# Single-row fetches shared between SyncE and ScalarE: twelve gathers instead of eight leave GpSimd, in step with the recurrence

## The chip, the cores and the metric

The kernel runs on one core of a Trainium2 chip. A core has five engines that run on their own and meet at semaphores: TensorE (PE in the profile) for matrix products, VectorE (DVE), ScalarE (ACT), GpSimd (POOL) and SyncE (SP), which here only issues transfers. SP and ACT issue plain transfers, each on a queue of its own, and GpSimd issues gathers; the bytes are moved by 16 DMA engines. The metric is the device time of one execution in microseconds. Time before: median 1851.0 us of three runs (1845.76 to 1854.84).

## The reference

A table `emb` has 100001 rows of 128 numbers; row 0 counts as zero. There are 1024 sequences of 50 item numbers, and a length for each.

```python
e = emb[seq]                              # (1024, 50, 128)
prefix = cumsum(e, axis=1)
denom = minimum(t_idx[None, :], lengths[:, None])
uF = prefix / denom[:, :, None]
y = (uF - uF.mean(axis=0)) * rsqrt(uF.var(axis=0) + BN_EPS) * gamma + beta
def step(v, x):                           # over the 50 places of the sequence
    v = v + (x - v) / 2
    spike = (v >= 1)
    return v - spike, spike
scores = mean_of_spikes @ emb.T           # (1024, 100001), float32
```

So there are 50 steps, each of which needs 1024 rows of the table at data-dependent places, and then one large product whose result, 410 MB, has to be written out.

## The kernel before

*Two stages.* The first stage is the loop over the 50 steps (line 383), with the state laid out as 128 features on the partitions by 1024 sequences. The second (line 546) goes over the table in pieces of 1024 rows, turns each piece round on PE, splits it into a high and a low part, multiplies it with the spike counts, and stores the scores. The second stage is untouched by the change. Most of the table pieces that the second stage begins with are fetched during the first one: `held` = 6 groups of 6 pieces and 4 more, 40 pieces of 512 KB, and of these 38 by SP at its very start (lines 231 to 238; the other two late, at line 473).

*One step.* `gather(t)` (line 244) fetches the 1024 rows of step t as eight indirect DMAs of 128 rows, issued by GpSimd into a tile `e` that has two buffers. `gather(t + 2)` stands behind step t's use of the buffer, so GpSimd can be two steps ahead, and then waits for PE. PE transposes the eight blocks of `e` and adds them onto the running sum `pre` in PSUM (line 390), after a small correction for row 0 (line 348). DVE makes the mean so far (`uF`, line 401) and its statistics (lines 402 and 410). ACT takes the square root of the variance (line 414) and centres `uF` (line 421), DVE finishes the reciprocal root (lines 427 to 440), ACT applies it (line 444), DVE makes the new potential `v` (line 447), and ACT writes `d`, the potential less the threshold (line 360), for the next step's reset. The square root of line 414 occurs once in each step, so its times give the periods of the steps.

*Rows by SP.* In the eight steps of `BY_SYNC` the last of the eight gathers is left out, and its 128 rows come by plain transfers of one row (512 bytes) each: `fetch_singles` (line 260) loads 32 row addresses into registers (line 265) and issues 32 transfers (line 268), four times over, into one of four banks of `held_rows`. PE takes that bank in place of the last block of `e` (line 392). The call for the next of these steps stands behind the use of the one before, in step order, but SP itself has nothing in its stream that ties it to the step, other than that a bank must have been read before it is filled again, four fetches later.

*What sets the order.* Each engine runs its own instructions in the order in which the program was written; the framework adds the semaphores. The completion of the transfers that SP and ACT issue is counted in eight semaphores, handed out in turn over both engines in the order of the program, and a transfer is issued only after the one that had its semaphore before, the eighth before it, has landed. GpSimd's gathers have eight of their own.

Of the kernel before, what the change touches and what calls it, by code (L numbers as in the profile page):

```python
# [17 lines left out]
U8 = mybir.dt.uint8  # L18
# [3 lines left out]
P = 128  # L22
# [4 lines left out]
BANK = 512  # L27
GROUP = 6
AHEAD = 6
# [3 lines left out]
SHIFT = TWICE + ASIDE  # L33
FURTHER = {5: 1, 6: 2}

BY_SYNC = (11, 17, 22, 28, 33, 38, 43, 48)
AT_ONCE = 32

SPARED = 120
PICKED = range(42, 97, 3)  # L40
# [7 lines left out]
def rec_kernel(  # L48
# [9 lines left out]
    nc = tc.nc  # L58
    B, T = seq.shape
    N, D = table.shape  # L60
    NB = B // P
# [16 lines left out]
    held_rows = const.tile([P, BANK], F32, tag="countB", name="held_rows")  # L78
# [16 lines left out]
    def pair(i):  # L95
        free.append([embp.tile([P, HALF], F32R, tag=f"{x}{i}", name=f"{x}_{i}") for x in ("hi", "lo")])

    def size(q):
        return min(HALF, N - q * HALF)
# [4 lines left out]
    def group(g):  # L104
        at = g if g < AHEAD else AHEAD - 2 + g % 2
        r = rowp.tile([P, GROUP, HALF], F32, tag=f"rows{at}", name=f"rows_{g}")
        for k in range(GROUP):
            rows[g * GROUP + SHIFT + k if g else k + ASIDE * (k >= TWICE)] = r[:, k, :]
        return r
# [19 lines left out]
    def pick(r, q, engine):  # L129
        j = PICKED.index(q)  # L130
        rows_of(r[:SPARED, :], picks, j)
        if j % 2:
            engine.dma_start(out=r[SPARED:, :], in_=runs[q * P + SPARED : (q + 1) * P, :])
            turn_by(TURN)
        else:
            turn_by(4)
            rows_of(r[SPARED:, :], ends, j // 2)
            turn_by(5)

    def fetch(r, k, q, n):  # L140

        engine = nc.sync if q < held else nc.scalar
        n = min(n, parts - q)
        whole = n - (size(q + n - 1) < HALF)
        wide = whole - (whole == n and q + whole - 1 in PICKED)
        if wide:
            engine.dma_start(
                out=r[:, k : k + wide, :],
                in_=table[q * HALF : (q + wide) * HALF, :].rearrange("(q p k) d -> p q (k d)", p=P, k=KQ),
            )  # L150
        if wide < whole:
            pick(r[:, k + wide, :], q + wide, engine)
        if whole < n:
            full, rest = divmod(size(parts - 1), KQ)
            c1 = (parts - 1) * HALF
            r = r[:, k + whole, :]
            if rest:
                at = full - full % 32
                nc.vector.memset(r[at : at + 32, :], 0.0)
                engine.dma_start(  # L160
                    out=r[full : full + 1, : rest * D],
                    in_=table[c1 + full * KQ : N, :].rearrange("(o k) d -> o (k d)", o=1),
                )
            if full:
                engine.dma_start(
                    out=r[:full, :],
                    in_=table[c1 : c1 + full * KQ, :].rearrange("(p k) d -> p (k d)", k=KQ),
                )
# [19 lines left out]
    def prepare(q, pt):  # L188
        turned(q, pt)
        split[q] = hi, lo = free.pop(0)  # L190
        vp, vh, vl = views(q, pt, hi, lo)
        nc.scalar.copy(vh, vp)  # L192
        nc.vector.tensor_tensor(vl, vp, vh.bitcast(F32), ALU.subtract)  # L193
# [18 lines left out]
    with ExitStack() as ph:  # L212
# [21 lines left out]
            rows[TWICE + k] = spare[:, k, :]  # L234
        fetch(spare, 0, TWICE, ASIDE)
        fetch(first, TWICE, SHIFT, GROUP - TWICE)
        for g in range(1, AHEAD):
            fetch(group(g), 0, g * GROUP + SHIFT, GROUP)

        es = {}

        def gather(t):
            es[t] = gp.tile([P, B], F32, tag="e", name=f"e_{t}")
            for n in range(NB - (t in BY_SYNC)):
                nc.gpsimd.indirect_dma_start(  # L247
                    out=es[t][:, n * P : (n + 1) * P],
                    out_offset=None,
                    in_=table,  # L250
                    in_offset=bass.IndirectOffsetOnAxis(ap=idx[:, n, t : t + 1].bitcast(U32), axis=0),
                )

        byte_rows = table.rearrange("n d -> (n d)").bitcast(U8)
        row_bytes = 4 * D
        starts = ids[:T, :P].bitcast(I32)
        regs = [nc.sync.alloc_register(f"row{k}") for k in range(AT_ONCE)]
        singles = {}

        def fetch_singles(i):  # L260
            t = BY_SYNC[i]
            rows_of = held_rows[:, i % (BANK // P) * P :][:, :P]
            singles[t] = rows_of
            for p0 in range(0, P, AT_ONCE):
                nc.sync.load(regs, starts[t : t + 1, p0 : p0 + AT_ONCE])  # L265
                for k, reg in enumerate(regs):
                    at = nc.sync.snap(reg, donate=True, min_val=0, max_val=(N - 1) * row_bytes)
                    nc.sync.dma_start(  # L268
                        out=rows_of[p0 + k : p0 + k + 1, :].bitcast(U8),
                        in_=byte_rows[bass.ds(at, row_bytes)].rearrange("(o b) -> o b", o=1),  # L270
                    )

        make_identity(nc, ident)
        isz = up.tile([P, NB, P], F32, tag="uF", name="isz")
        rb = up.tile([P, NB, P], F32, tag="uF", name="rb")
        gather(0)

        last_ids = ids[:, P : P + T]
        nc.vector.tensor_copy(last_ids, idx[:, NB - 1, :])
        ips = vp.tile([P, B], F32, tag="v0", name="ips")  # L280
        nc.tensor.transpose(ips[:T, :P], last_ids, ident)
        nc.vector.tensor_scalar_mul(starts, ips[:T, :P], float(row_bytes))
        fetch_singles(0)

        nc.vector.memset(isz, 0.0)
        for u in (0, P // 2):
# [46 lines left out]
        def only(t):  # L333

            k = t % ONLY
            if k == 0:
                n = min(ONLY, T - t)
                nc.vector.tensor_tensor(
                    ls[:, :n, :],
                    r0n.unsqueeze(1).to_broadcast([P, n, D]),  # L340
                    sel[:, t : t + n].unsqueeze(2).to_broadcast([P, n, D]),
                    ALU.mult,
                )
            return ls[:, k, :]
# [12 lines left out]
        def over(t, v):  # L357

            d = lp.tile([P, B], BF16, tag="d", name=f"d_{t}")
            nc.scalar.activation(d, v, AF.Identity, bias=less)  # L360
            return d
# [4 lines left out]
        def spiked(out, cs, v):  # L366
            nc.vector.scalar_tensor_tensor(out, v, V_TH, count[:, cs], ALU.is_ge, ALU.add)
# [15 lines left out]
        for t in range(T):  # L383
# [18 lines left out]
                nc.vector.bn_stats(bs[:, h, :], uF[:, cs])  # L402
            if t + 2 < T:
                gather(t + 2)
            if t in BY_SYNC[:-1]:
                fetch_singles(BY_SYNC.index(t) + 1)
            if not last:
                correct(t + 1, l)
            mv = sp.tile([P, 2], F32, tag="mv", name=f"mv_{t}")
# [3 lines left out]
            r = sp.tile([P, 1], F32, tag="r", name=f"r_{t}")  # L413
# [29 lines left out]
            def x(vt, cs):  # L443
                nc.scalar.activation(vt, uF[:, cs], AF.Identity, bias=hgb[:, 1:2], scale=a)

            def step(vt, cs):
                nc.vector.scalar_tensor_tensor(vt, negv[:, cs], -0.5, vt, ALU.mult, ALU.add)  # L447

            if not last:
                vt = vp.tile([P, B], F32, tag=f"v{(t + 1) % 2}", name=f"v_{t}")  # L450
                x(vt, whole)
                if t:
                    spiked(count, whole, v)
                step(vt, whole)
                v = vt
                if t == T - 2:
                    spiked(count, whole, v)
                    moved = once.tile([P, P], F32, tag="r0hi", name="moved")
                    nc.vector.tensor_scalar_add(moved, v[:, pieceA], beta2)
                    near = once.tile([P, P], F32, tag="r0", name="near")  # L460
                    nc.vector.scalar_tensor_tensor(near, v[:, pieceA], V_TH, moved, ALU.is_ge, ALU.subtract)
                d = over(t, v)
                if t + 2 < T:
                    l = only(t + 2)

                if t in (T - 8, T - 6):
                    q = (t - T + 8) // 2
                    pair(q)
                    prepare(q, vp.tile([P, HALF], F32, tag="v0", name=f"pt_{q}"))
                    if q == TWICE - 1:  # L470
                        for k in range(TWICE):
                            rows[GROUP + ASIDE + k] = first[:, k, :]
                        nc.sync.dma_start(
                            out=first[:, :TWICE, :],
                            in_=table[(GROUP + ASIDE) * HALF : (GROUP + SHIFT) * HALF, :].rearrange(
                                "(q p k) d -> p q (k d)", p=P, k=KQ
                            ),
                        )

# [64 lines left out]
    for c, W in enumerate(WIDTHS):  # L546
# [38 lines left out]
        for n, q in blockwise:  # L585
# [4 lines left out]
            o = os[n]  # L590
# [27 lines left out]
            if n in (1, 4) and c >= MIDDLE and to_fetch < parts:  # L618
                g, k = divmod(to_fetch - SHIFT, GROUP)
                if k or to_split >= (g - 1) * GROUP + SHIFT:  # L620
                    if k == 0:
                        r = group(g)
# [23 lines left out]
```

## Time and profile before

| | |
|---|---|
| median of the runs | 1851.0 us (1845.76, 1851.0, 1854.84) |
| the profiled execution | 1852.0 us, its span 1850.0 us |
| mean granted clock of TensorE | 0.763 |
| busy over the span: PE, DVE, ACT, POOL | 58%, 51%, 36%, 23% |
| gathers of line 247 | 392 |
| single-row transfers of line 268 | 1024, by SP |
| HBM read, written | 77.69 MB, 409.60 MB |

How to read it. The page cuts the span into 40 slices and gives the busy share of each engine in tenths. A group's row has its line, engine and operation, the tiles that it writes and reads, how often it ran, its busy time and the mean of one, and the time that its engine stood before it with what ended that. A row for one line gives the shortest, median and longest of its instructions in ns and the first and last start in us. A wait's row gives who waited for whom, the total in us, how often, and the longest. A stretch's row gives, after its length, busy us and counts of PE, PEld, DVE, ACT and POOL, then the granted clock, the busy share of the DMA engines and the GB/s that they moved. A row in order of time gives start and duration in us; SPq and ACTq are the queues on which SP and ACT issue transfers.

### The profile page before, as it was taken

What the parts mean: (1) busy time and instruction counts of PE and PEld (TensorE: products, weight loads), DVE (VectorE), ACT (ScalarE), POOL (GpSimd) and SP (SyncE); (2) the same over time, 40 slices, a digit from 0 to 9 for tenths busy, and PEclk for the clock granted to TensorE, in tenths of its full rate; (3) what the DMA queues carried; (4) which work ended last, traced back from release to release, by engine and by line L of the source; (5) the groups of instructions that cost most, each with busy time, mean ns of one, the idle gap of its engine ahead of it and who ended that gap; (6) DMA issues with size and microseconds to landing.
All of it is one profiled execution on the core that took longest, in us unless ns stands there. A gap on an engine that the chain in (4) does not pass through costs nothing.

```text
span 1850.0 us, 14486 instructions
## 1 busy us (share of the span) xinstructions
PE 1070.6 (58%) x4465; PEld 810.4 (44%) x4465; DVE 947.7 (51%) x1128; ACT 674.2 (36%) x698; POOL 429.7 (23%) x459
## 2 busy tenths in 40 slices
PE   3321302120212213088998988878888878888984
PEld 2110201010101112066676766666666666666763
DVE  4653707261524346175566655555555555555652
ACT  2331303130312123054555544444444444444542
POOL 6664716262716254200000000010010010000000
PEclk7555555555555555589999999999889899989998
DMA  9511101010201011069999999999999999999999
GB/s 351 178 44 28 49 15 46 21 48 16 50 14 45 17 41 32 15 266 413 405 422 402 431 421 426 425 427 428 426 427 427 426 427 428 423 422 429 427 428 391
DMA packets 54993, 488.27 MB, mean 264 GB/s; under 512 B 12719, under 2 KB 14000, under 8 KB 33796
## 3 DMA queue, kind: packets, MB, share of 16 engines
q1 hardware_dynamic: 32944, 431.39, 55.4%
q0 software_dynamic: 16560, 35.40, 6.6%
q10 hardware_dynamic: 5412, 20.56, 2.7%
q8 instruction: 35, 0.57, 0.1%
q14 instruction: 42, 0.34, 0.1%
HBM read 77.69 MB, written 409.60 MB: 263 GB/s over the span
## 4 chain that ended last, share of the span: by engine, by line
DMA 33%; PE 15%; DVE 4%; ACT 3%; SPq 3%; issue 3%; ACTq 0%; DVEq 0%
DMA scores<-o 33%; PE po L200 15%; DVE o L601 2%; ACT o L603 2%; SPq L268 2%; DVE pairs L193 1%; ACT pairs L192 1%; PE pt L176 0%; SPq L265 0%; ACT hi L192 0%; DVE lo L193 0%; DVE bs L402 0%; DVE uF L401 0%; DMA held_rows<-in_L_rec_emb_table 0%; ACTq L603 0%
## 5 line engine op out<-in xcount | busy, mean ns | idle before, releaser
L601 DVE TENSOR_SCALAR o<-po 128x1024 f32<-128x1024 f32 (+1 forms) x390 | 467.2, 1214 | 309.6 <-DMA scores<-o 163.7
L603 ACT ACTIVATE o<-po 128x1024 f32<-128x1024 f32 x392 | 393.2, 1025 | 490.7 <-DMA scores<-o 337.2
L247 POOL DMA_INDIRECT e<-in_L_rec_emb_table,idx x392 | 372.9, 951 | 377.2 <-PE pre L390 218.6
L200 PE MATMUL po<-pairs,countB 128*128 128x512 f32 (+1 forms) x1120 | 289.9, 404 | 47.8 <-ACT o L603 47.6
L200 PE MATMUL po<-pairs,countC 128*128 128x512 f32 (+1 forms) x840 | 243.9, 438 | 62.3 <-ACT o L603 55.4
L401 DVE SCALAR_TENSOR_TENSOR uF<-rlen,pre 128x512 f32<-128x512 f32 x100 | 67.9, 679 | 399.0 <-PE pre L390 317.2
L200 PEld LDWEIGHTS po<-pairs,countB 128*128 128x128 f32 x1120 | 208.3, 191 | 110.9 <-ACT o L603 64.9
L200 PEld LDWEIGHTS po<-pairs,countC 128*128 128x128 f32 x840 | 169.8, 210 | 115.9 <-ACT o L603 66.0
L348 PE MATMUL pre<-zT,ls 128*128 128x512 f32 x100 | 78.5, 787 | 227.3 <-DVE uF L401 136.7
L390 PE MATMUL pre<-ident,held_rows 128*128 128x128 f32 x8 | 3.6, 447 | 349.2 <-DMA held_rows<-in_L_rec_emb_table 349.2
L414 ACT ACTIVATE r<-mv,eps 128x1 f32<-128x1 f32 x50 | 14.8, 295 | 509.2 <-DVE mv L410 406.3
L122 POOL DMA_INDIRECT rows<-in_L_rec_emb_table,picks x19 | 18.6, 981 | 685.2 <-PE pt L176 681.9
L390 PEld LDWEIGHTS pre<-ident,held_rows 128*128 128x128 f32 x8 | 1.5, 183 | 351.7 <-issue 351.7
L348 PEld LDWEIGHTS pre<-zT,ls 128*128 128x128 f32 x100 | 29.4, 295 | 267.4 <-DVE uF L401 159.3
L193 DVE TENSOR_TENSOR pairs<-pt,pairs 128x1024 fp32r<-128x1024 f32 x70 | 85.3, 1218 | 98.0 <-ACT pairs L192 97.1
L390 PE MATMUL pre<-ident,e 128*128 128x128 f32 x392 | 101.3, 422 | 19.2 <-DMA e<-in_L_rec_emb_table,idx 12.7
L176 PE MATMUL pt<-ident,rows 128*128 128x128 f32 (+1 forms) x768 | 104.9, 282 | 9.3 <-DVE v L447 5.0
L176 PEld LDWEIGHTS pt<-ident,rows 128*128 128x128 f32 (+1 forms) x768 | 94.3, 147 | 26.3 <-issue 10.8
L390 PEld LDWEIGHTS pre<-ident,e 128*128 128x128 f32 x392 | 81.6, 219 | 37.4 <-DMA e<-in_L_rec_emb_table,idx 18.9
L200 PE MATMUL po<-hi,countB 128*128 128x512 f32 x208 | 84.8, 408 | 10.8 <-ACT o L603 9.2
L192 ACT CAST pairs<-pt 128x1024 fp32r<-128x1024 f32 x70 | 70.0, 1012 | 39.2 <-PE pt L176 39.2
L200 PE MATMUL po<-lo,countB 128*128 128x512 f32 x208 | 83.3, 401 | 0.0
(99 smaller groups left out, 1110.1 us busy)
## 6 DMA issues: line engine op xcount, KB each, us to landing
scores<-o SPq DMA_DIRECT2D x96, 3072.0 KB
scores<-o SPq DMA_DIRECT2D x32, 1536.0 KB
scores<-o SPq DMA_DIRECT2D x29, 1024.0 KB
scores<-o SPq DMA_DIRECT2D x8, 2896.5 KB
rows<-in_L_rec_emb_table ACTq DMA_DIRECT2D x19, 1024.0 KB
held_rows<-in_L_rec_emb_table SPq DMA_DIRECT2D x1024, 0.5 KB
rows<-in_L_rec_emb_table SPq DMA_DIRECT2D x5, 3072.0 KB
e<-in_L_rec_emb_table,idx POOLq DMA_INDIRECT x392
```

Of the source, the lines that this page charges most:

```text
L122: nc.gpsimd.indirect_dma_start(out=r, out_offset=None, in_=runs, in_offset=bass.IndirectOffsetOnAxis(ap=which[: r.shape[0], j : j + 1].bit ...
L176: nc.tensor.transpose(pt[:, k0 : k0 + pw], r[:pw, k0 : k0 + D], ident[:pw, :pw])
L192: nc.scalar.copy(vh, vp)
L193: nc.vector.tensor_tensor(vl, vp, vh.bitcast(F32), ALU.subtract)
L200: nc.tensor.matmul(po[:, :kw], lhsT=counts[n], rhs=part[:, k0 : k0 + kw], start=j == 0, stop=j == 1,)
L247: nc.gpsimd.indirect_dma_start(out=es[t][:, n * P : (n + 1) * P], out_offset=None, in_=table, in_offset=bass.IndirectOffsetOnAxis(ap=idx[: ...
L268: nc.sync.dma_start(out=rows_of[p0 + k : p0 + k + 1, :].bitcast(U8), in_=byte_rows[bass.ds(at, row_bytes)].rearrange("(o b) -> o b", o=1),)
L348: nc.tensor.matmul(pre[h], lhsT=l, rhs=zT[:, h * BANK : (h + 1) * BANK], start=t == 0, stop=False, skip_group_check=True,)
L390: nc.tensor.matmul(pre[h][:, k : k + P], lhsT=singles[t] if h * BANK + k + P == B and t in singles else e[:, h * BANK + k : h * BANK + k + P],
L401: nc.vector.scalar_tensor_tensor(uF[:, cs], rlen[:, cs], 1.0 / (t + 1), pre[h], ALU.max, ALU.mult)
L601: nc.vector.tensor_scalar_mul(o[:, h0 : h0 + hw], po[:, :hw], 1.0 / T)
L603: nc.scalar.mul(o[:, h0 : h0 + hw], po[:, :hw], 1.0 / T)
```

## The change

Twelve steps instead of eight leave their last gather out: 6, 10, 14 and so on to 46, and 49. Their rows are cut into batches of 32, four for each such step, 48 in all, and one batch is issued at the end of each of steps 0 to 47: SP loads 22 addresses and issues 22 rows, ACT loads 10 addresses and issues 10 rows, and in the program's order they stand in turns, SP, ACT, SP, ACT, until ACT's ten are through. Of the table pieces only groups 0 and 1 and the two pieces set aside are fetched at the start; groups 2 to 5 become 24 parts of one piece each, and SP issues one behind each of the first 24 batches. The batch of a step stands behind everything else of that step: on ACT behind the activation of line 360, and ahead of the next step's square root. In step 44 it stands behind the load of line 473.

```diff
-BY_SYNC = (11, 17, 22, 28, 33, 38, 43, 48)
-AT_ONCE = 32
+APART = (*range(6, 47, 4), 49)
+STARTED = 0
+SYNC_ROWS, OWN_ROWS = 22, 10
+EARLY = 2
...
-        for g in range(1, AHEAD):
+        for g in range(1, EARLY):
             fetch(group(g), 0, g * GROUP + SHIFT, GROUP)
+        parts_left = []
+        for g in range(EARLY, AHEAD):
+            r = group(g)
+            parts_left += [(r, k, g * GROUP + SHIFT + k, 1) for k in range(GROUP)]
...
-            for n in range(NB - (t in BY_SYNC)):
+            for n in range(NB - (t in APART)):
...
-        regs = [nc.sync.alloc_register(f"row{k}") for k in range(AT_ONCE)]
+        sync_regs = [nc.sync.alloc_register(f"row{k}") for k in range(SYNC_ROWS)]
+        own_regs = [nc.scalar.alloc_register(f"own{k}") for k in range(OWN_ROWS)]
...
-        def fetch_singles(i):
-            t = BY_SYNC[i]
-            rows_of = held_rows[:, i % (BANK // P) * P :][:, :P]
-            singles[t] = rows_of
-            for p0 in range(0, P, AT_ONCE):
-                nc.sync.load(regs, starts[t : t + 1, p0 : p0 + AT_ONCE])
-                for k, reg in enumerate(regs):
...
+        def fetch_row(engine, reg, row):
+            at = engine.snap(reg, donate=True, min_val=0, max_val=(N - 1) * row_bytes)
+            engine.dma_start(
+                out=row.bitcast(U8),
+                in_=byte_rows[bass.ds(at, row_bytes)].rearrange("(o b) -> o b", o=1),
+            )
+
+        def fetch_some(i, p0):
+            t = APART[i]
+            rows_of = singles[t] = held_rows[:, i % (BANK // P) * P :][:, :P]
+            p1 = p0 + SYNC_ROWS
+            nc.sync.load(sync_regs, starts[t : t + 1, p0:p1])
+            nc.scalar.load(own_regs, starts[t : t + 1, p1 : p1 + OWN_ROWS])
+            for k, reg in enumerate(sync_regs):
+                fetch_row(nc.sync, reg, rows_of[p0 + k : p0 + k + 1, :])
+                if k < OWN_ROWS:
+                    fetch_row(nc.scalar, own_regs[k], rows_of[p1 + k : p1 + k + 1, :])
+
+        todo = [(i, p0) for i in range(len(APART)) for p0 in range(0, P, SYNC_ROWS + OWN_ROWS)]
...
-        fetch_singles(0)
...
-            if t in BY_SYNC[:-1]:
-                fetch_singles(BY_SYNC.index(t) + 1)
...
+                if t >= STARTED and todo:
+                    fetch_some(*todo.pop(0))
+                    if parts_left:
+                        fetch(*parts_left.pop(0))
```

More of the change, by code (lines that the diff above doesn't have):

```diff
@@ L256, in rec_kernel @@
         starts = ids[:T, :P].bitcast(I32)
-        regs = [nc.sync.alloc_register(f"row{k}") for k in range(AT_ONCE)]
+        sync_regs = [nc.sync.alloc_register(f"row{k}") for k in range(SYNC_ROWS)]
+        own_regs = [nc.scalar.alloc_register(f"own{k}") for k in range(OWN_ROWS)]
         singles = {}
-        def fetch_singles(i):
-            t = BY_SYNC[i]
-            rows_of = held_rows[:, i % (BANK // P) * P :][:, :P]
-            singles[t] = rows_of
-            for p0 in range(0, P, AT_ONCE):
-                nc.sync.load(regs, starts[t : t + 1, p0 : p0 + AT_ONCE])
-                for k, reg in enumerate(regs):
[L267 to L271, printed above, removed]
+        def fetch_row(engine, reg, row):
[15 more added lines that the diff above has]
+        todo = [(i, p0) for i in range(len(APART)) for p0 in range(0, P, SYNC_ROWS + OWN_ROWS)]
         make_identity(nc, ident)
```

## The prediction

> **What bounds the kernel now.** I read the slices of the page first, then the groups and waits of the step stage, then the row transfers of line 268 in stretches.
>
> ```profile
> span 1850.0 us, 14486 instructions
> DVE  4653707261524346175566655555555555555652
> POOL 6664716262716254200000000010010010000000
> DMA  9511101010201011069999999999999999999999
> L414 ACT ACTIVATE r<-mv,eps 128x1 f32<-128x1 f32 x50 | 14.8, 295 | 509.2 <-DVE mv L410 406.3
> ```
>
> A slice is 46 us. From slice 17 on DMA is full: that is the stage of products and stores, which the change leaves alone. Before it stand fifty steps in which DMA is nearly idle, and DVE and POOL stop several times together, in holes a slice or two wide. The ends of this stage come from the square root that every step has once on ACT:
>
> ```profile
> L414 ACT ACTIVATE r<-mv,eps x50: 294/295/298, 22.5 to 798.2; 128x1 f32<-128x1 f32 x50
> 789.04 0.30 ACT L414 ACTIVATE r<-mv,eps 128x1 f32<-128x1 f32 x1 [42.19 <-DVE mv L410]
> ```
>
> Step 0 is at 22.5, step 48 at 789.0, step 49 at 798.2 us. The 48 periods between step 0 and step 48 take (789.0 - 22.5)/48 = 16.0 us each. What they wait for is in the table of waits and in the record of line 268:
>
> ```profile
> PE pre L390 <- DMA held_rows<-in_L_rec_emb_table: 349.2, 8, 50.5
> POOL e L247 <- PE pre L390: 218.6, 10, 36.7
> SPq L268 <- DMA held_rows<-in_L_rec_emb_table: 5.7, 12, 0.8
> L268 SPq DMA_DIRECT2D held_rows<-in_L_rec_emb_table x1024: 1/228/5427, 42.0 to 785.1; - x171
> ```
>
> Eight times, once for each gather that SP does by single rows, PE stands up to 50.5 us for those rows, and GpSimd stands behind PE. SP issues its 1024 rows without a rest from 42.0 to 785.1 us: 743/1024 = 0.73 us a row. SP's issuing bounds the stage. Its rows hardly wait for earlier rows (5.7 us in all), and DMA is idle, so it is the issuing itself that is slow, and not always:
>
> ```profile
> L268 SPq DMA_DIRECT2D held_rows<-in_L_rec_emb_table x29: 227/228/229, 165.3 to 174.3; - x29
> 165.50:174.50 9.00, 0.00 (x0) 0.00 (x0) 0.00 (x0) 0.00 (x0) 0.00 (x0) 0.50 0.01 2
> ...
> L268 SPq DMA_DIRECT2D held_rows<-in_L_rec_emb_table x19: 3/228/715, 179.8 to 189.2; - x19
> 180.00:190.20 10.20, 3.67 (x12) 2.21 (x10) 9.51 (x17) 5.02 (x6) 7.42 (x8) 0.50 0.19 47
> ...
> L268 SPq DMA_DIRECT2D held_rows<-in_L_rec_emb_table x30: 3/228/727, 380.8 to 419.5; - x30
> 380.00:420.00 40.00, 9.20 (x29) 6.12 (x28) 21.17 (x37) 10.99 (x13) 27.32 (x29) 0.50 0.19 48
> L268 SPq DMA_DIRECT2D held_rows<-in_L_rec_emb_table x52: 227/228/263, 441.2 to 460.0; - x52
> ```
>
> Each pair is the rows that SP issued in a stretch, and beside it the busy times there (the last of them POOL's). With GpSimd still, 29 rows in 9.0 us: 0.31 us a row. In the first ten microseconds of a burst of gathers, 19 rows in 10.2 us. In a long run of gathers, 30 rows in 40 us: 1.33 us a row. In 20 us almost without gathers (the 52 rows), 0.385 us with the register loads in it. So GpSimd's gathers slow SP's issue by up to four times, with a few rows' grace after each rest. What it is that they share, the trace does not show.
>
> **The change, part by part.** It removes four gathers of 392 (eight were gone already, now twelve are) and adds 512 rows.
>
> ```profile
> L247 POOL DMA_INDIRECT e<-in_L_rec_emb_table,idx x392 | 372.9, 951 | 377.2 <-PE pre L390 218.6 <-issue 114.7 <-remote 32.7
> 380.13 0.94 POOL L247 DMA_INDIRECT e<-in_L_rec_emb_table,idx  x1 [0.30 <-issue]
> L265 SPq TENSOR_LOAD <-ids x32: 21/2127/2329, 39.7 to 772.8; - x32
> ...
> 3.57 0.47 SPq L147 DMA_DIRECT2D spare<-in_L_rec_emb_table  x1
> ```
>
> *GpSimd.* A gather takes 0.94 + 0.30 = 1.25 us. Steps 0 to 47 issue 388 - 16 = 372 of them, 7.75 a step: 9.7 us a step, against 372 + 4 before. By itself this saves 4 x 1.25 = 5 us.
>
> *SP.* In each of 48 steps it loads 22 registers instead of 32 at a time (2.127 x 22/32 = 1.5 us), issues 22 rows, and in half of the steps a table part, which costs it one more issue (0.47 us, the last row here), 0.24 us on average. Its rows go from 1024 to 1056, so if their pace stayed, nothing would be won. The pace need not stay, because of the order. The framework hands eight completion semaphores to the transfers of SP and ACT in turn, in the program's order, and each transfer waits for the one eight before it. With SP's and ACT's rows in turns, SP can be no more than about a step ahead of ACT, and ACT is tied to its step. So instead of running free while the steps stand for 50 us, SP is paced once a step, and each step in which SP is late holds back the next gathers too: the burst of 9.7 us is followed by a rest, each time.
>
> One end: every burst finds SP rested, as at 180 us. Load and part take 1.7 of the 9.7 us, the other 8.0 us give 8.0 x 19/10.2 = 14.9 rows, and the last 7.1 take 7.1 x 0.31 = 2.2 us after the burst: a step of 11.9 us. Other end: the short rest repairs nothing, and the pace is that of the long run: 9.7/1.33 = 7.3 rows in the burst, and 14.7 x 0.385 + 0.24 = 5.9 us for the others: 15.6 us. I take 13.5, a little under the middle, as the order forces a rest in each step.
>
> [...]
>
> *ACT.* It issues, behind the last activation of each step, a load of 10 registers (2.127 x 10/32 = 0.7 us) and ten rows. No row of before shows ACT issuing a single row; it issues table loads later on:
>
> ```profile
> 378.91 1.11 ACT L360 ACTIVATE d<-v,less 128x1024 bf16<-128x1024 f32 x1 [1.30 <-issue]
> 374.44 0.30 ACT L414 ACTIVATE r<-mv,eps 128x1 f32<-128x1 f32 x1 [2.50 <-DVE mv L410]
> 381.84 0.29 ACT L414 ACTIVATE r<-mv,eps 128x1 f32<-128x1 f32 x1 [1.82 <-DVE uF L401]
> ...
> 1092.54 1.01 ACT L192 CAST pairs<-pt 128x1024 fp32r<-128x1024 f32 x1 [0.78 <-PE pt L176]
> 1092.55 0.43 ACTq L147 DMA_DIRECT2D rows<-in_L_rec_emb_table  x1
> ```
>
> The last pair shows ACT issuing while its activation computes, so the rows can begin when L360 begins. From there to the next square root is 381.84 - 378.91 = 2.93 us, in a step of 381.84 - 374.44 = 7.40 us. The price of ACT's row lies between 0.31 us (SP's without gathers) and 1.33 us (SP's in a long run of them); 0 is excluded, as ACT's stream is in order. At 0.31 the load and ten rows take 3.8 us, the step 7.40 - 2.93 + 3.8 = 8.3 us, under GpSimd's 9.7: hidden. I take that end, since ten rows after a rest is what SP shows at 180 us. If it stands bare, the square root, and DVE's reciprocal behind it, wait for every microsecond over 9.7. The wait that the turns add (ACT's first rows for the last rows of SP's step before) has the same square root queued behind it; a step of 13.5 us holds it.
>
> *Table parts.* SP's start loads 14 tiles instead of 38, and 24 follow with the batches.
>
> ```profile
> 20.00:40.00 20.00, 8.84 (x23) 3.65 (x21) 12.84 (x24) 7.31 (x8) 15.12 (x17) 0.62 1.03 389
> 4.08 35.58 SPq L147 DMA_DIRECT2D rows<-in_L_rec_emb_table  x6
> L473 SPq DMA_DIRECT2D rows<-in_L_rec_emb_table x1: 410/410/410, 785.5 to 785.5; - x1
> ```
>
> At 389 GB/s a part of 0.52 MB keeps DMA for 1.35 us, and rows on SP's queue land behind it: between 0 and 24 x 1.35 = 32 us, of which I take 0, since a step has 13.5 us for it. The early crowd that kept SP at the table loads until about 40 us goes away, but step 0 stays near 22.5 us: its own gathers set that. The load of line 473 is passed: it stood behind all rows (785.5 us); now the rows of the last four steps stand behind it, and it waits for PE in step 44: between 0 and 22 x 0.31 = 6.8 us, I take 0.
>
> *Sum.* Step 48 comes at 22.5 + 48 x 13.5 = 670.5, step 49 another 9.2 us later (798.2 - 789.0), at 679.7 instead of 798.2: 118.5 us less. The profiled execution took 1852.0 us (span 1850.0 and 2.0 around it), 1 us over the median of the runs, 1851.0. 1852.0 - 118.5 = 1733.5 us. The ends of SP's price give this case's own range: 11.9 us puts step 49 at 602.9, 1657 us; 15.6 at 780.5, 1834 us.
>
> **The rivals.**
>
> *Faster, GpSimd binds.* If rows paced by the step are never slowed, a step is the 9.7 us of its gathers: 22.5 + 466 + 9.2 = 497 us, and 1551 us in all. For it: 22 rows at 0.31 and the load are 8.3 us. Against it: already the first ten microseconds of a burst gave only 19 rows.
>
> *One channel behind both queues.* If what the gathers slow lies behind SP and ACT together, the second issuer adds nothing and 32 rows share one pace: 9.7 x 19/10.2 = 18 rows in the burst and 14 x 0.31 = 4.3 us after it, 14.1 us, or by the long run 7.3 rows and 24.7 x 0.31 = 7.7 us, 17.4; the middle, 15.8, puts step 49 at 790 us: 1844, no change within what can be told. For it: the rows wait for nothing of SP's own. Against it: DMA is at 0.19. [...]
>
> *Slower: ACT's rows on the path.* If ACT's rows cost what SP's do in a long run of gathers, load and rows take 0.7 + 13.3 = 14.0 us before each square root: 7.40 - 2.93 + 14.0 = 18.5 us a step, step 49 at 920 us, 1974 us. It decides from the point where the step passes 16.0 us: (16.0 - 4.47 - 0.7)/10 = 1.08 us a row. For it: every row that ACT issues has the whole step behind it, where SP had nothing. Against it: when ACT is late the gathers stop, and rows are cheap again.
>
> *Not what it says.* The words tell of twelve gathers, but eight had left: were only the four counted, the gain would be the 5 us above, inside the noise. The rest hangs on the order, as worked out.
>
> **How the numbers follow.** 0.60 for the forecast, 0.10 for GpSimd binding, 0.13 for one channel (0.02 of it faster, 0.06 within the bound, 0.05 slower), 0.17 for ACT. What a measurement here can tell from no change is about 0.5%, 9 us (the three runs lie 9 us apart). Faster: 0.60 + 0.10 + 0.02 = 0.72; the same: 0.06; slower: 0.17 + 0.05 = 0.22. The range leaves out the 0.10 below and the further half of the rival above: 1640 to 1930 us.
>
> **What would show it.** Right: square roots 12 to 15.6 us apart in steps 1 to 48, evenly, without holes of 50 us; no long wait of PE for held_rows; GpSimd resting 2 to 6 us in every step. SP's step wrong: the same holes as now, or no rest of GpSimd. ACT's term wrong: the square root waiting on ACT's own queue, with ACT's rows 1 us or more apart. If the stage of stores took other than the 1052 us that it has now, the forecast would be wrong in a place that I hold to be untouched.

## The result and the profile after

The changed kernel takes 1867.8 us (median of six runs, 1863.4 to 1870.6) beside 1850.0 us for the kernel before (1845.8 to 1855.4): a ratio of 1.0089, 95% interval 1.0065 to 1.0114. It is slower by 0.9%; the forecast was 1733.5 us. One thing has to be known for all that follows: the kernels were compared on six occasions, and on two of them the kernel before took 1552 us instead of 1835 to 1850, so each comparison below names the time of the kernel before beside it.

The first lines of the page of after, in 40 slices:

```profile
span 1868.5 us, 15620 instructions
DVE  4353634454354436446566655555456555555652
POOL 6453633553364435200000000010010010010000
DMA  5122222221111111139999999999999999999999
```

The wide holes of before are gone, but slices with little work are still there, and DMA becomes full in the same slice as before, of a longer span. The square root of each step (line 426 now) in time order, in a stretch and at the end; the bracket is the time that ACT stood before it and what ended that:

```profile
252.95 0.30 ACT L426 ACTIVATE r<-mv,eps 128x1 f32<-128x1 f32 x1 [20.40 <-DVE mv L422]
264.14 0.29 ACT L426 ACTIVATE r<-mv,eps 128x1 f32<-128x1 f32 x1 [5.61 <-DMA held_rows<-in_L_rec_emb_table]
277.99 0.29 ACT L426 ACTIVATE r<-mv,eps 128x1 f32<-128x1 f32 x1 [8.87 <-DMA held_rows<-in_L_rec_emb_table]
293.57 0.29 ACT L426 ACTIVATE r<-mv,eps 128x1 f32<-128x1 f32 x1 [10.59 <-DMA held_rows<-in_L_rec_emb_table]
318.59 0.30 ACT L426 ACTIVATE r<-mv,eps 128x1 f32<-128x1 f32 x1 [20.01 <-DVE mv L422]
...
790.05 0.30 ACT L426 ACTIVATE r<-mv,eps 128x1 f32<-128x1 f32 x1 [4.88 <-DMA held_rows<-in_L_rec_emb_table]
816.79 0.29 ACT L426 ACTIVATE r<-mv,eps 128x1 f32<-128x1 f32 x1 [19.91 <-DVE mv L422]
```

Three periods of 11.2, 13.9 and 15.6 us, then one of 25.0: a hole in one step of four, 65.6 us for the four. Step 0 is at 22.5 and step 48 at 790.05, so the mean period is (790.05 - 22.5)/48 = 16.0 us, to a tenth that of before. Step 49 comes at 816.8, where it came at 798.2. The 18.6 us between them are the whole difference: what follows took 1868.5 - 816.8 = 1051.7 us, before 1051.8.

The waits of the stage, and the rows and the loads of SP and ACT:

```profile
PE pre L404 <- DMA held_rows<-in_L_rec_emb_table: 323.1, 12, 30.3
POOL e L254 <- PE pre L404: 260.6, 15, 27.7
SPq L270 <- DMA held_rows<-in_L_rec_emb_table: 17.4, 31, 2.8
```

```profile
L270 SPq DMA_DIRECT2D held_rows<-in_L_rec_emb_table x1056: 1/228/3776, 7.3 to 813.1; - x176
L270 ACTq DMA_DIRECT2D held_rows<-in_L_rec_emb_table x480: 3/224/1413, 28.9 to 789.8; - x160
L279 SPq TENSOR_LOAD <-ids x48: 13/1850/1970, 5.3 to 804.3; - x48
L280 ACTq TENSOR_LOAD <-ids x48: 1446/2381/2446, 26.4 to 784.1; - x48
```

PE still waits 323 us for single rows, now twelve times. SP issues without a rest again, from 7.3 to 813.1 us, 805.8/1056 = 0.76 us a row (before 0.73), and step 49 comes 3.7 us behind its last row. SP's rows are what the steps wait for, as before.

### The profile page after: what moved, and what is told of

It reads as the page before. It is cut to its first block, busy times and chain, and to the rows that moved or that the text cites. A ratio compares the mean times of both kernels' runs of the same rounds, so it can differ in the third digit from the quotient of the medians.

```text
span 1868.5 us, 15620 instructions
## 1 busy us (share of the span) xinstructions
PE 1060.5 (57%) x4465; PEld 807.2 (43%) x4465; DVE 949.8 (51%) x1128; ACT 674.1 (36%) x698; POOL 424.7 (23%) x455
## 4 chain that ended last, share of the span: by engine, by line
DMA 34%; PE 14%; DVE 4%; ACT 3%; issue 2%; SPq 2%; ACTq 0%; DVEq 0%
DMA scores<-o 33%; PE po L202 14%; DVE o L618 3%; ACT o L620 2%; SPq L270 1%; DVE pairs L195 1%; PE pt L178 1%; ACT pairs L194 1%; SPq L279 0%; DMA held_rows<-in_L_rec_emb_table 0%; ACT hi L194 0%; ACTq L270 0%; DVE lo L195 0%; ACTq L280 0%; ACT v L456 0%
## 5 line engine op out<-in xcount | busy, mean ns | idle before, releaser
L254 POOL DMA_INDIRECT e<-in_L_rec_emb_table,idx x388 | 367.8, 948 | 410.3 <-PE pre L404 260.6
L426 ACT ACTIVATE r<-mv,eps 128x1 f32<-128x1 f32 x50 | 14.7, 295 | 550.3 <-DMA held_rows<-in_L_rec_emb_table 264.4
L404 PE MATMUL pre<-ident,held_rows 128*128 128x128 f32 x12 | 5.4, 447 | 323.1 <-DMA held_rows<-in_L_rec_emb_table 323.1
L124 POOL DMA_INDIRECT rows<-in_L_rec_emb_table,picks x19 | 18.6, 981 | 676.4 <-PE pt L178 673.6
L439 DVE RECIPROCAL r<-r 128x1 f32<-128x1 f32 x50 | 8.1, 163 | 190.7 <-issue 97.9
L404 PE MATMUL pre<-ident,e 128*128 128x128 f32 x388 | 94.6, 420 | 5.7 <-issue 3.2
L202 PE MATMUL po<-hi,countB 128*128 128x512 f32 x208 | 84.6, 407 | 11.0 <-ACT o L620 9.5
L404 PEld LDWEIGHTS pre<-ident,e 128*128 128x128 f32 x388 | 81.5, 222 | 16.3 <-issue 12.8
```

Of the source, the lines that this page charges most:

```text
L124: nc.gpsimd.indirect_dma_start(out=r, out_offset=None, in_=runs, in_offset=bass.IndirectOffsetOnAxis(ap=which[: r.shape[0], j : j + 1].bit ...
L202: nc.tensor.matmul(po[:, :kw], lhsT=counts[n], rhs=part[:, k0 : k0 + kw], start=j == 0, stop=j == 1,)
L254: nc.gpsimd.indirect_dma_start(out=es[t][:, n * P : (n + 1) * P], out_offset=None, in_=table, in_offset=bass.IndirectOffsetOnAxis(ap=idx[: ...
L404: nc.tensor.matmul(pre[h][:, k : k + P], lhsT=singles[t] if h * BANK + k + P == B and t in singles else e[:, h * BANK + k : h * BANK + k + P],
```

## The experiments

Theory G, formed on this comparison: a gather costs SP a fixed loss of its issuing time wherever it falls, about 1 us. Take SP's rows at 0.32 us each (22 rows that start from 372.7 to 379.5 us, without gathers: 6.8 us for 21 gaps), its loads at their median, its 24 table parts at 0.37 us each, and its waits as the table of waits has them; what is left of its issuing span, divided by the gathers that started within it, is the loss. Before: 743.1 - 1024 x 0.32 - 32 x 2.13 - 5.7 = 341.5 us over 362 gathers, 0.94 us. After: 805.8 - 1056 x 0.32 - 48 x 1.85 - 8.9 - 31.5 = 338.7 us over 385, 0.88 us. (5.7 and 31.5 us are the waits, 8.9 us the parts.)

**Without rows, and without gathers.** Four kernels, on an occasion on which the kernel before took 1551.8 us; all but the first were executed once.

```diff
all_gathers
-APART = (*range(6, 47, 4), 49)
+APART = ()
one_gather
-            for n in range(NB - (t in APART)):
+            for n in range(1):
sync_all
-SYNC_ROWS, OWN_ROWS = 22, 10
+SYNC_ROWS, OWN_ROWS = 32, 0
no_act_rows
-                if k < OWN_ROWS:
-                    fetch_row(nc.scalar, own_regs[k], rows_of[p1 + k : p1 + k + 1, :])
```

In one_gather PE reads the first gather's block in place of the others, in all_gathers the table parts stay behind the steps, and in sync_all and no_act_rows ACT's load goes too; no_act_rows has zeros in the places of ACT's rows.

> No row goes by SP or ACT: all eight gathers of each step are on GpSimd, the table parts stay behind the steps. Theory G (each gather holds up an issuer of rows for about 1.0 us, and SP's issuing bounds the steps; from SP's 806 us for 1056 rows at 0.31 us, 48 loads at 1.85 us and 24 parts, the rest over 377 gathers): with no rows to issue a step is 8 x 1.25 = 10.0 us, the last step's square root at 22.5 + 48 x 10.0 + 9.2 = 512 us instead of 817, 1563 us in all. Rival R1 (GpSimd's gathers bind, and rows taken off it help): twelve gathers more at 1.25 us, about 1883 us.

> The ten rows of each batch that ACT fetched are left out (their places hold zeros), SP's 22 stay. Theory G (each issuer is held up for itself): SP needs its 806 us as before, the steps stay at 16 us, 1868 us within 1%. Rival R2 (SP and ACT share one channel that the gathers slow): 480 of 1536 rows less, so SP's loss of some 380 us falls by about 119 us, 1750 us.

> Only the first of a step's eight gathers is made, and PE reads its block in place of the others; all rows by SP and ACT stay. Theory G: SP needs 22 x 0.31 + 1.85 + 0.2 + 1.0 = 9.9 us a step, ACT's chain 7.4 - 2.9 + 2.4 + 3.1 = 10.0 us; last square root near 512 us, 1563 us in all, and rows 0.3 us apart throughout. Rival R3 (rows are slow because of their own number or their waits for one another): steps stay at 16 us, about 1868 us.

> All 32 rows of a batch by SP, none by ACT; the rest as in the changed kernel. Theory G: SP needs 48 x (32 x 0.31 + 2.13 + 0.2) + 377 x 1.0 = 965 us instead of 806, about 2026 us. Rival R2 (one channel behind both): the rows only change their queue, about 1868 us.

Measured: all_gathers 1560.1 us, ratio 1.0055 (1.0038 to 1.0072); no_act_rows 1546.6, one_gather 1696.8, sync_all 1704.7 us. On this occasion the loss was nearly absent. The rows of sync_all:

```profile
L270 SPq DMA_DIRECT2D held_rows<-in_L_rec_emb_table x1536: 227/228/3175, 7.7 to 648.3; - x192
```

By them 640.6 - 1536 x 0.32 - 48 x 2.14 - 8.9 - 14.4 = 23.1 us over 384 gathers are 0.06 us. So the numbers of theory G for no_act_rows and sync_all (1868, 2026) missed, and so did its 1563 for one_gather: even with only 50 gathers left the kernel of the change takes 1697 us. The kernel without ACT's rows is the quickest, 1546.6 us, with no step over 12.5 us. What the loss does can be seen only where the kernel before is slow, as in the next two groups of runs.

**The same, and the changed kernel whole, where the kernel before takes 1835 and 1847.5 us.** Theory L, in the expectations from here on, lays the time to the tie between the two queues, and not to the gathers alone. parts_first is the changed kernel with `EARLY = AHEAD`, all table parts at the start.

> The changed kernel itself, whole. In the last comparison the kernel before took 1551.8 us instead of 1850, and rows beside gathers were issued at nearly their lone pace, so the price of a row beside gathers seems to belong to the occasion. Theory G (a gather costs SyncE about 1.0 us of its row issue): where the kernel before takes 1850 us, 1868 here, ratio 1.009. Theory L (the two queues' rows wait for one another's completions, and ScalarE's load and rows lie in its chain): where the kernel before takes 1552 us, the step is 9.85 us in three of four and about 20 in the fourth, as with one gather a step, and the whole about 1700 us, ratio 1.095. Rival: there the holes go, 1552 to 1560 us.

> The kernel before, whole, for its trace on this occasion. Theory: either 1850 us with 1.0 us lost by SyncE per gather and a step of 16.0 us, or 1552 us with under 0.15 us lost per gather and a step of 10.0 us that GpSimd's eight gathers fill. Rival: 1552 us with SyncE still behind, so that the time is saved elsewhere than in the steps.

> All 400 rows' gathers by GpSimd, no single rows; table parts behind the steps. Theory G: 1560 us on either occasion, since no row is issued that gathers could hold up: ratio 0.843 where the kernel before takes 1850, 1.0055 where it takes 1552. Rival (the occasion slows the gathers or the clock, not the rows): 1850 or more beside 1850.

> The changed kernel with all table parts fetched at the start, none between batches. Theory G or L: within 0.5% of the changed kernel on the same occasion (24 issues of about 0.36 us are 9 us of SyncE's time, less those of the fewer whole fetches; SyncE sets the end where rows are slow: up to 9 us less there). Rival (the parts between the batches hold SyncE's queue back): 30 us or more less than the changed kernel.

Measured beside 1835.0 us: the changed kernel 1862.2, ratio 1.0162 (1.0134 to 1.0190); parts_first 1855.8, 1.0112 (1.0077 to 1.0147), so the parts behind the batches cost some 6 us and no more; all_gathers_2 1625.6, 0.888 (0.885 to 0.891). The last beats both kernels by far here: with the rows gone the stage is rid of SP. Theory G's 1560 us was missed by 65 us all the same, so something is lost here besides SP's time for rows.

> As one_gather: only the first gather of each step is left, its block serves the step's others, so that GpSimd sends 50 gathers in place of 388. Theory G, where the kernel before takes some 1840 us: without gathers beside them the rows cost what they cost on the quicker occasion, 1697 us again, 165 less than the changed kernel; SyncE still sets the end by its waits for ScalarE's rows. Rival (on that occasion every row is slow, gathers or not): 1850 us or more. Where the kernel before takes 1552 us: 1697 again, nothing new.

> As no_act_rows: ScalarE's load and its ten rows of each batch are left out, zeros in their places. Theory G, where the kernel before takes some 1840 us: SyncE's own sum stays, 1056 rows at 0.32 us, 48 loads, 385 gathers at 1.0 us, its last row at about 810 us, 1865 us in all. Theory L (the two queues hold each other up): the rows of ScalarE are what slows SyncE's, 1750 us or less. Where the kernel before takes 1552 us: 1547 again.

> As sync_all: SyncE fetches all 32 rows of each batch, ScalarE none. Theory G, where the kernel before takes some 1840 us: 1536 rows at 0.32 us, 48 loads of 2.14 us and 385 gathers at 1.0 us put the last row at about 985 us, 2040 us in all. Theory L: with no second queue the loss per gather falls, 1750 to 1870 us. Where the kernel before takes 1552 us: 1705 again.

> The changed kernel, whole, once more. Where the kernel before takes some 1840 us: 1862 us, ratio 1.009 to 1.016. Where it takes 1552 us: theory L, 1700 us (the ScalarE rows in the chain make the step 9.85 us, and SyncE's lag a hole of about 10 us in one step of four), ratio 1.095; theory G alone, 1570 us (SyncE's sum with 0.13 us per gather is 478 us, less than the steps').

Measured beside 1847.5 us: one_gather_2 1700.2, no_act_rows_2 1813.1, sync_all_2 1996.3, the changed kernel 1868.0 us (1.0107, 1.0081 to 1.0133). The record of line 270 in one_gather_2:

```profile
L270 SPq MOVE held_rows<-in_L_rec_emb_table x1056: 29/29/29, 7.3 to 642.8; - x176
```

and in the changed kernel (its first trace), SP's two lines in each of two stretches, the first without a gather and the second with thirteen:

```profile
L270 SPq DMA_DIRECT2D held_rows<-in_L_rec_emb_table x23: 227/228/263, 305.0 to 314.9; - x23
L270 SPq MOVE held_rows<-in_L_rec_emb_table x22: 29/29/29, 307.6 to 314.9; - x22
...
L270 SPq DMA_DIRECT2D held_rows<-in_L_rec_emb_table x22: 2/228/737, 333.3 to 350.7; - x22
L270 SPq MOVE held_rows<-in_L_rec_emb_table x21: 3/29/704, 334.0 to 350.6; - x21
```

A MOVE stands ahead of each transfer and is none itself. Without gathers it takes 29 ns each time, beside them up to 704 ns here: what is held up is SP's instructions, not the transfer alone. With 50 gathers left the kernel takes 1696.8 us on the first occasion and 1700.2 on this one. So the loss is the gathers' doing, as G says and its rival does not.

```profile
L270 SPq DMA_DIRECT2D held_rows<-in_L_rec_emb_table x1056: 1/228/3648, 7.4 to 763.0; - x176
PE pre L402 <- DMA held_rows<-in_L_rec_emb_table: 371.9, 12, 36.0
...
L270 SPq DMA_DIRECT2D held_rows<-in_L_rec_emb_table x1536: 1/228/3572, 7.6 to 947.1; - x192
```

That is no_act_rows_2 and, in the last line, sync_all_2. In no_act_rows_2 the steps without a hole are shorter, the holes longer (36.0 us), and SP's last row comes only 50 us sooner: ACT's rows do not bind, SP's do. The loss is (755.6 - 337.9 - 88.8 - 8.9 - 14.8)/385 = 0.79 us a gather, so ACT's rows add some 0.1 us to it. sync_all_2 ends its rows at 947.1: (939.5 - 491.5 - 101.7 - 8.9 - 17.4)/384 = 0.83. G's sum holds in form (2040 forecast, 1996 measured), but its 1.0 us a gather is too high where ACT has no rows: no_act_rows_2, at 1813, lies about halfway between G's 1865 and L's 1750.

**A rest in each step, by force.** The prediction's step rests on rests of GpSimd that the traces do not show. Here VectorE copies one column of a batch's 32 rows in the next step, before it combines the statistics, so no step goes on without them.

```diff
+            if fetched:
+                nc.vector.tensor_copy(seen[fetched[1] : fetched[1] + SYNC_ROWS + OWN_ROWS, :], fetched[0])
+                fetched = None
             mv = sp.tile([P, 2], F32, tag="mv", name=f"mv_{t}")
...
-                    fetch_some(*todo.pop(0))
+                    i, p0 = todo.pop(0)
+                    fetch_some(i, p0)
+                    fetched = singles[APART[i]][p0 : p0 + SYNC_ROWS + OWN_ROWS, :1], p0
```

> The changed kernel, and in each step VectorE first copies a column of the 32 rows of the step before, so that no step goes on without its rows and GpSimd's gathers must pause in every step. Theory P (the step of the prediction: a rest in each step gives SyncE its grace back), where the kernel before takes some 1840 us: steps of 12 to 15.6 us, the end near 1733 us. Theory G (each gather costs SyncE 0.9 to 1.0 us wherever the rests fall): 22 rows at 0.32 us, a load of 1.6, a share of a part of 0.2 and 7.75 gathers at 1.0 us are 16.6 us a step, step 49 at about 829 us, 1880 us in all. Where the kernel before takes 1552 us: 10.5 us a step by G with 0.13 us a gather, about 1590 us.

> The changed kernel, whole, beside the run above. Where the kernel before takes some 1840 us: 1862 us. Where it takes 1552 us: theory L, 1700 us by ScalarE's rows in the chain and SyncE's lag; theory G alone, 1570 us.

Measured beside 1847.8 us: tied 1784.7 us, ratio 0.965 (0.962 to 0.968); the changed kernel 1867.8, 1.0097 (1.0076 to 1.0119). One wait more makes the kernel 83 us faster than the change without it; the forecasts were 1733 us by the prediction's step and 1880 by G. The square roots of tied (line 431) and SP's record there:

```profile
242.18 0.29 ACT L431 ACTIVATE r<-mv,eps 128x1 f32<-128x1 f32 x1 [8.65 <-DVE mv L427]
256.24 0.29 ACT L431 ACTIVATE r<-mv,eps 128x1 f32<-128x1 f32 x1 [8.47 <-DVE seen L424]
270.21 0.30 ACT L431 ACTIVATE r<-mv,eps 128x1 f32<-128x1 f32 x1 [8.38 <-DVE seen L424]
284.89 0.29 ACT L431 ACTIVATE r<-mv,eps 128x1 f32<-128x1 f32 x1 [9.09 <-DVE seen L424]
298.80 0.30 ACT L431 ACTIVATE r<-mv,eps 128x1 f32<-128x1 f32 x1 [8.32 <-DVE mv L427]
```

```profile
L270 SPq DMA_DIRECT2D held_rows<-in_L_rec_emb_table x1056: 1/228/3638, 7.3 to 720.3; - x176
SPq L270 <- DMA held_rows<-in_L_rec_emb_table: 71.6, 49, 3.7
```

The periods are even, 12.8 to 14.8 us, but for those that end at steps 1, 44 and 45 (35.1, 19.2 and 23.5 us). SP's waits come to 84.6 us (71.6, a table load's 6.8 behind PE, and small ones), and its loss is (713.0 - 337.9 - 89.7 - 8.9 - 84.6)/385 = 0.50 us a gather. By an estimate that lets the gathers within SP's waits hold up nothing of SP's, at one gather in 1.25 us these are at most 84.6/1.25 = 68; without them the loss is 191.9/317 = 0.61 us, and that of the changed kernel, counted the same way, 338.7/360 = 0.94. So G as I put it falls too: the loss is not the same wherever the rests fall. With a rest in each step it is little more than half, or two thirds by the second count.

**The changed kernel where the kernel before takes 1551.9 us.**

> The changed kernel, whole. Where the kernel before takes some 1840 us: 1866 us, ratio 1.01. Where it takes 1552 us: 1700 us by theory L (ScalarE's load and rows in its chain, SyncE's lag in one step of four), 1570 us by theory G alone.

> The changed kernel with each step waiting for the 32 rows of the step before. Where the kernel before takes some 1840 us: 1785 us again, steps of about 14 us. Where it takes 1552 us: with rows at their lone pace a step is ScalarE's chain of 9.85 us or GpSimd's 9.7, some 10.5 us with the wait: about 1590 us, under the changed kernel there if that is 1700.

Measured: the changed kernel 1708.7 us, ratio 1.1014 (1.0993 to 1.1036); tied_2 1735.9, 1.1187 (1.1165 to 1.1209). The changed kernel's lines here, and in the last two rows tied_2's:

```profile
221.55 0.30 ACT L426 ACTIVATE r<-mv,eps 128x1 f32<-128x1 f32 x1 [5.21 <-DMA held_rows<-in_L_rec_emb_table]
244.70 0.29 ACT L426 ACTIVATE r<-mv,eps 128x1 f32<-128x1 f32 x1 [18.16 <-DVE mv L422]
255.50 0.30 ACT L426 ACTIVATE r<-mv,eps 128x1 f32<-128x1 f32 x1 [5.21 <-DMA held_rows<-in_L_rec_emb_table]
```

```profile
L270 SPq MOVE held_rows<-in_L_rec_emb_table x1056: 29/29/29, 7.3 to 654.4; - x176
SPq L270 <- DMA held_rows<-in_L_rec_emb_table: 156.3, 97, 6.0
PE pre L404 <- DMA held_rows<-in_L_rec_emb_table: 233.1, 12, 23.6
...
L270 SPq DMA_DIRECT2D held_rows<-in_L_rec_emb_table x1056: 227/228/3388, 7.3 to 671.6; - x176
SPq L270 <- DMA held_rows<-in_L_rec_emb_table: 187.5, 98, 5.5
```

No MOVE is held up, though the gathers are all there, and the holes stay. Theory L was near (1700 us): SP now waits 156 us for the landing of rows that hold its semaphores, and the step in four without its rows takes some 20 to 23 us. Without ACT's load and rows (no_act_rows, beside 1551.8 us) the holes were gone and the kernel took 1546.6 us. tied_2 missed its 1590 us: nearly all its steps are 12.4 to 14.7 us long here too, though SP's loss is absent: (664.2 - 337.9 - 89.9 - 8.9 - 209.3)/385 = 0.05 us a gather. In the list of instructions SP's last rows of a batch stand behind the landing of ACT's, which come at the step's end. So the forced wait has a chain of its own of some 13 us, and most of tied's 14 us on the other occasion can be that chain, not the price of rows.

## Why the prediction was wrong, step by step

**The bound was named rightly.** SP's issuing set the stage before, and sets it after. That gathers slow SP's rows is borne out by one_gather_2 (1700.2 us beside 1868.0); that rests win some of it back, by the smaller loss in tied (0.50 us a gather for 0.88).

**The step that failed: "I take 13.5, a little under the middle, as the order forces a rest in each step."** The order forces none. The rows issued by 330 us in the changed kernel of the prediction, and in tied:

```profile
L270 SPq DMA_DIRECT2D held_rows<-in_L_rec_emb_table x374: 1/228/3776, 7.3 to 329.7; - x187
L270 ACTq DMA_DIRECT2D held_rows<-in_L_rec_emb_table x190: 3/224/726, 28.9 to 329.7; - x190
```

```profile
L270 SPq DMA_DIRECT2D held_rows<-in_L_rec_emb_table x444: 2/228/3638, 7.3 to 329.6; - x148
L270 ACTq DMA_DIRECT2D held_rows<-in_L_rec_emb_table x200: 6/224/716, 28.9 to 323.5; - x100
```

In after ACT has issued 190/10 = 19 batches and SP 374/22 = 17; in tied both are at 20. The prediction reasoned from the order of the source, in which SP's and ACT's rows of the same batch stand in turns. In the trace of after SP's and ACT's transfers have eight semaphores between them, and most wait for their own (1074 of 1263 and 473 of 510); in the source's order ACT's rows would so also have waited for SP's of their own batch, and the next square root, behind ACT's rows, for both. The framework hands out the eight semaphores in an order of its own. The numbers of the semaphores that the trace holds for each transfer, followed in their turn, show it: but for the first batches, ACT's rows of a batch stand beside SP's of the one to three batches before. ACT's row 191 stands behind SP's row 374, which is where the two are at 330 us. So the steps could go on with SP up to three batches behind, until PE asked for the last of four. Gathers therefore ran in trains over three steps, PE then stood 27 us (323.1/12), and SP got its rests in those holes, as before. The forecast's 13.5 us stand for a loss of (648 - 337.9 - 88.8 - 8.9)/372 = 0.57 us a gather. With forced rests the measured loss is 0.50, with the order as it is 0.88. The size was about right for rests that were not there. One thing is not taken apart: the wait in tied also changed the order of the transfers, and its semaphores have ACT's rows beside SP's of the same batch. Whether that order alone, without the wait, would have forced the rests was not tried.

**The other end was at hand.** The prediction's price for a rest that repairs nothing was 15.6 us; 16.0 came. Step 49 comes 18.6 us later than before, which the terms of SP's sum give: it starts at 7.3 instead of 42.0 us (-34.7), has 32 rows more (+10.2), 48 loads of 1.85 in place of 32 of 2.13 (+20.6), 24 parts (+8.9), 23 more gathers within its span, at the lower loss of each (-2.8 in all, 338.7 for 341.5), and 25.8 us more of waits. That is +28.0 at SP's last row (813.1 for 785.1); 9.4 of it come back as step 49 is now itself the last that waits.

**ACT's term was mis-sized, without setting the time on this occasion.** "At 0.31 the load and ten rows take 3.8 us, the step ... 8.3 us ... hidden": the rows did cost about that where nothing slowed them (ten in 3.3 to 3.6 us in tied_2), but the load takes 2.38 us by its median instead of 0.7. In one_gather most steps without a hole take 9.7 to 10.1 us, at or over GpSimd's 9.7. In the changed kernel ACT's ten rows were slowed as well, and the square root waited for ACT's own queue (264.4 us in 31 waits in the table of waits). no_act_rows_2 shows what that was worth: 55 us, since SP's lag takes up most of it. Where the loss is absent ACT's load and rows, with the tie that they bring, did set the time: 1708.7 us with them, 1546.6 without. SP's load of 22 registers took 1.85 us, not 1.5: 10 registers more (32 for 22) cost 2.13 - 1.85 = 0.28 us, 28 ns each, which by an estimate leaves a fixed part of 1.85 - 22 x 0.028 = 1.2 us. ACT's median of 2.38 us for ten is far over that line: by the estimate, ten would take 1.2 + 10 x 0.028 = 1.5. Of the 48, 39 started within 0.04 us of the activation of line 374, which takes 1.11 us, and took 2.35 to 2.45 us; the three that started 0.94 to 0.98 us behind it took 1.45 to 1.48, near SP's line; one that started 2.27 us behind it took 2.38 again. What sets its length is not taken apart.

**The rivals.** The time was nearest to that of "one channel behind both queues" (1844), but its mechanism did not carry it: sync_all_2 is 128 us slower than the changed kernel, so the second issuer does take rows off SP. All the same, in a stretch of after SP's and ACT's instructions come in turns, about 0.70 us each, as the last section shows. "ACT's rows on the path" showed in three steps of four and was not the bound. The table parts and line 473 were rightly put near nothing (parts_first: 6 us).

What stays open is why a gather slows SP's and ACT's instructions on some occasions and not on others. It does not follow the granted clock: the kernel before took 1550.3 to 1553.9 us in seven executions at mean granted clocks of 0.81 to 0.96, beside tied 1842.5 to 1858.4 us in thirteen at 0.76 to 0.96, and before_again, one execution, took 1827.8 us at 0.968, nine tenths or more in every slice but two (below). It is not the chip alone: on one chip the kernel before took 1551.8 us on one occasion and 1847.8 on another. Which of its cores ran is not on record.

```profile
span 1825.9 us, 14486 instructions
PEclk9999999999999999999999999989999999999998
```

## What to carry to other kernels

Here the semaphores that two queues share tied them in the order in which the framework hands them out, which was not the order of the source: one queue could fall three batches behind the other (ACT's row 191 stood behind SP's row 374). A pace that relies on rests needs a wait that forces them: tied took 1784.7 us beside 1867.8 for the change without its wait, though 1735.9 beside 1708.7 where the kernel before took 1552. A chain that one engine issues without a rest is costed as a sum over the whole stage (rows, loads, loss per gather), and the sum of before says at once whether moving rows about changes any term. Before single rows are spread over more engines, the kernel without them is worth a run: here 400 plain gathers took 1625.6 us where the two kernels took 1835 and 1862, and 1560 where the kernel before took 1552.

## What the runs showed of the hardware

On the occasions with the loss, more is held up than the row issuers. In all_gathers no single row is issued, and yet the stage took 572 us on one occasion and 508 on the other. What VectorE waited for, on the slower of the two and then on the quicker:

```profile
DVE uF L415 <- remote: 134.4, 23, 10.0
```

```profile
DVE uF L415 <- PE pre L404: 107.2, 48, 2.7
```

On the slower one it stood up to 10.0 us at a time for a signal whose sender the profile does not name, while PE's matmuls before it had long started (one such wait ends at 48.5 us, and the last of these matmuls starts at 39.7). In a stretch of after in which SP's rows are slow, the list of instructions shows SP and ACT taking turns at about 0.70 us an instruction, MOVE and transfer alike: SP's start at 36.21, 37.64, 39.04 and 40.45 us, ACT's at 36.92, 38.35, 39.75 and 41.15. What makes them take turns no run here took apart.
